# A convolution, Fourier and feed-forward block: the first normalisation's factors from transposes and statistics instructions, their placing by small DMAs, the gate products in five

## The chip, the cores and the metric

The kernel runs on one core of one Trainium2 chip. A core has five engines that run their own instruction queues in order and meet at semaphores: TensorE (PE, matrix products; weight loads are listed apart as PEld), VectorE (DVE), ScalarE (ACT), GpSimd (POOL) and SyncE (SP), which here only issues DMAs. SBUF is the working memory of 128 partitions, PSUM the memory that PE writes its results to. The metric is the device time of one execution in microseconds. The kernel before takes 7428.37 us, the median of 3 runs (7425.02 to 7429.1).

## The reference, cut to what matters

The input is 64 images of 96 channels and 56 x 56 pixels. Per image:

```
# layer 0: convolution
out = silu(bn(expand_w @ x))                  # 96 -> 192 channels
out = channel_shuffle(shift_groups(out), 4)
dw  = bn(depthwise3x3(out)) + bn(out * id_w)
out = silu(bn(dw))
se  = mean(out over pixels)                   # squeeze and excite, 12 groups
se  = sigmoid(exp_w . relu(red_w . se + red_b) + exp_b)
x   = silu(bn(proj_w @ (out * se)) + x)       # 192 -> 96 channels
# layer 1: tokens t = x as [3136 pixels, 96]
n   = (t - mean(t)) / sqrt(var(t) + 1e-5)     # first normalisation, over the channels
h   = relu(bn(n @ w1.T))                      # 192 channels
X   = fft(h over the pixels); complex relu with diagonal r, i; y = real(ifft)
t   = t + bn(y @ w2.T)
n   = (t - mean(t)) / sqrt(var(t) + 1e-5)     # second normalisation
t   = t + qlinear(relu(qlinear(n)))           # 96 -> 384 -> 96, rounded to 8 and 16 bits
```

The change concerns the first normalisation, the squeeze-and-excite gate and the order of all the work.

## The kernel before, in words

One image is one batch `b`. Its work is cut into small functions ("steps", listed in `STEPS`), each for one engine: `ea_mm` to `eb_ev` expand the channels from the padded image `x`, `dw_mm`/`dw_ev` and `lt`/`ls` do the depthwise convolution (on PE for 128 channels, on DVE for the other 64), `se1_mm` to `se2_pw` the gate, `pj_mm` to `pj_ev` the projection with the residual, which writes the tokens to one of three buffers `t`, channels on the partitions. `c_mm` to `sp_ev` are the first normalisation, `w1_mm`/`w1_ev` the first linear layer, `f1`, `f2`, `w2`, `i1`, `i2` the Fourier stage and its way back into `t`, `n_mm` to `x_ev` the second normalisation, `h_*` and `o_*` the feed-forward layer and the output.

The order is written out by hand in a table: `PLAN` gives every step and part of it a time within a batch, from about -152 to 302, and the program records all steps of all 64 batches sorted by `b * PERIOD + time`:

```
for _, b, k, i in sorted((b * PERIOD + when, b, k, i) for b in range(NB) ...):
    STEPS[k](b, i)
```

The times only sort. Each engine executes its own steps in that order, as early as their operands and buffers allow; a PERIOD of 116.13 doesn't hold the kernel to 116.13 us a batch. About four batches are in work at once.

Buffers that make steps wait: PSUM has two large buffers `psa`, used in turn by `w1`, `f1`, `f2`, `w2`, `i1`, `i2`, and four banks `psb` for all others; a bank is free again when the reader of its last tile is done. The image `x` (in SBUF) is one buffer, so rows of the next image are loaded (`x_in`, seven parts of eight rows, each two DMAs) when the projection has read the old ones. `rs_full`, the table of the factors, is one buffer too.

The first normalisation in the kernel before. Mean and factor are not applied to the tokens. `w1c` holds the weights with the centring folded in, the bias is in its row 48 (GAP), and row 48 of `t` gets the deviation of each token, so that the product plus bias comes out multiplied by the deviation; `w1_ev` multiplies by the reciprocal deviation from `rs_full`. For that:

- `c_mm` (L594, through `centred`, L575 to 583): for each of 7 groups of 4 x 112 tokens, a product of the tokens with the 96-column centring table, in two column tiles of 64 and 48 tokens. 56 products a batch.
- `c_sq` (L597, `squared`, L587) squares on ACT, `c_v` (L600, `variance`, L591 and L592) sums on DVE and scales, `c_pow` (L609) takes the power -1/2 on POOL, all by group.
- `sp_v` (L616) makes the deviations, for 16 and for 12 columns of 112 tokens. `sp_mm` turns them into rows by a product with the unit matrix `eye` (L623), and spreads the reciprocals over 128 partitions by two products with the selecting table `sel` (L626). `sp_ev` copies both out of PSUM and stores the deviations to row 48 of `t` with a small DMA (L635).

The second normalisation (`n_mm` to `n_x`) uses the same helpers `centred`, `squared` and `variance` and isn't changed.

The gate: `sums_of(b)` has nine columns of channel sums: four for each half of the image, for 128 channels in four groupings, and one for the other 64. `se1_mm` (L501) accumulates nine products with `rd_w`. `se2_mm` makes the 192 gate values in the layout that the projection wants, for 4 groupings of 32 channels, each four times over the partitions: 16 products of 32 rows (L516) and two of 64 (L524).

Of the kernel before, what the change touches and what calls it, by code (L numbers as in the profile page):

```python
# [15 lines left out]
C = 96  # L16
HW = 56
# [24 lines left out]
PERIOD = 116.1319138  # L42
PLAN = {
    "x_in": (-152.0645309, -141.2993712, -141.6679729, -127.3567477, -140.4175705, -140.8791946, -144.4420607),
    "ea_mm": (-135.7474068, -125.9928362, -122.8659980, -92.0913164, -104.6229276, -112.7267047, -105.2043967),
    "ea_ev": (-126.2515393, -125.9319230, -118.0983755, -90.4041115, -101.0728895, -111.5980423, -102.3613406),
    "eb_mm": (-111.6980332, -109.8791967, -100.7140648, -97.1962889, -100.1521321),
    "eb_ev": (-110.3732416, -105.7335079, -96.1257152, -94.4046805, -98.4601370),
    "dw_mm": (-82.7821446, -82.7811446, -81.0068981, -63.1375564, -61.9034126, -61.9024126),
    "dw_ev": (-77.0167479, -77.0167407, -77.0167341, -77.0167381, -60.0783737, -60.0901315, -61.6632225, -61.9014126),  # L50
    "lt": (
        -94.1171461, -91.0376475, -90.8110105, -84.2097398, -83.7232133, -81.4803127, -80.9974894, -76.5785475,
        -74.8117188,
    ),
    "ls": (-64.8543731,),
    "se1_mm": (-59.5055097,),
    "se1_ev": (-59.5045097,),
    "se2_mm": (-50.8239976,),
    "se2_ev": (-50.8229976,),
    "se2_th": (-49.7520464,),  # L60
    "se2_pw": (-44.5741770,),
    "pj_mm": (-42.5731636, -41.7287092, -36.7747065, -35.6782576),
    "pj_add": (
        -40.2650446, -40.2796225, -38.9333258, -40.2483174, -35.5690602, -35.5880423, -35.6772576, -33.4761964,
    ),
    "pj_ev": (-40.2419829, -40.2697824, -38.5536557, -39.8652465, -34.0027180, -34.0500919, -35.3385576, -32.9440877),
    "c_mm": (-25.3931448, -24.9391274, -22.9549349, -19.1090370, -21.8289396, -16.1784897, -12.8300748),
    "c_sq": (-24.0734158, -22.3310211, -21.2158857, -15.9717527, -16.5706079, -9.4527160, -10.1829185),
    "c_v": (-23.2641412, -18.5309510, -18.4395411, -12.1303106, -14.6345003, -8.6082441, -9.9996125),
    "c_pow": (-20.9452270, -13.7085425, -15.6301869, -11.4052805, -5.5266851, -7.5286825, -8.6183219),  # L70
    "sp_v": (-10.4956685, -0.4576308),
    "sp_mm": (-8.7178013, 0.9602487),
    "sp_ev": (-8.0803778, 4.1899488),
    "w1_mm": (1.8276103, -4.3293031, 1.4017277, 17.3741797, 5.8433199, 12.9915551, 9.4140075, 15.5299552),
    "w1_ev": (3.6555094, 1.6165891, 1.9120628, 20.7312269, 9.6265414, 15.0156650, 13.8227102, 19.8352916),
    "f1_mm": (21.4014670, 24.1096820, 21.6576037, 26.6862219, 27.4741769, 27.9467307),
    "f1_ev": (
        22.2675762, 22.3170374, 26.0226358, 25.8913366, 23.5344234, 24.6372460, 27.5678865, 27.6926244, 28.0977988,
        28.0983444, 28.8837920, 29.1288017,
    ),  # L80
    "f2_mm": (32.9716451, 29.2956139, 40.4533546, 44.1808546, 54.3439615, 55.8928972),
    "f2_u": (
        34.7148069, 35.1913156, 34.1757328, 34.5592467, 43.6172965, 44.2134504, 47.8768609, 48.4841614, 54.8402044,
        56.0332668, 59.7855946, 59.8827469,
    ),
    "f2_s": (
        37.7742909, 38.9626044, 36.3314048, 38.2311950, 49.1716883, 51.9368525, 50.9287577, 52.8460367, 57.5441738,
        59.9906303, 63.3144177, 64.6228680,
    ),
    "f2_r": (39.1150665, 38.5882242, 53.2778442, 54.0205100, 60.9052003, 68.4340083),  # L90
    "f2_p": (42.7834619, 39.8243535, 54.3731261, 54.5511382, 74.7679031, 77.0928815),
    "w2_mm": (65.3220254, 72.7056746, 74.7689031, 77.5437437),
    "w2_ev": (74.4448721, 74.9963870, 78.9222540, 80.2832661),
    "i1_mm": (80.9444124, 84.7640673, 88.5170591),
    "i1_ev": (82.2893126, 88.4629084, 91.9656135),
    "i2_mm": (95.7640245, 96.2774235, 108.3942264, 108.5026333),
    "i2_ev": (97.9070222, 99.2818561, 103.4147153, 107.9237827, 111.1146537, 111.4580718, 116.1401610, 115.7667382),
    "n_mm": (108.3281033, 107.0253359, 111.0518458, 120.4450658, 127.6246107, 127.0848414, 135.0039327),
    "n_sq": (108.8298534, 107.7986165, 117.6335593, 121.4070884, 128.9291689, 129.7921415, 135.5665766),
    "n_v": (109.1993497, 108.7476571, 118.3787911, 123.1793589, 128.9779128, 132.9514515, 137.6454231),  # L100
    "n_pow": (109.3967291, 109.1646949, 118.7377401, 123.8157957, 129.4982271, 133.4035466, 138.6999285),
    "n_x": (109.5403406, 109.6506044, 121.7562605, 124.9580100, 130.6758534, 134.0609417, 138.7110927),
    "x_mm": (109.8231134, 116.4694255, 122.0874878, 125.5477824, 134.5799192, 137.9526790, 139.7016670),
    "x_ev": (114.5600886, 118.9508230, 124.0625718, 126.2314751, 135.6759825, 140.9016708, 141.4110371),
    "h_mm": (
        141.6399550, 141.5117830, 141.4989540, 144.1173694, 144.1040402, 144.1151174, 156.6711686, 171.5607898,
        157.1121049, 172.3447607, 173.0555422, 181.3723226, 173.4712447, 192.1075898, 192.1283063, 199.7145424,
        199.3278846, 211.5886849, 203.8560342, 211.0696281, 205.6897160,
    ),
    "h_ev": (  # L110
        142.0485799, 142.2676534, 143.4387889, 146.2975891, 147.7127555, 145.5174570, 158.9476510, 171.7019227,
        158.8458276, 172.3457607, 176.0278841, 187.9388941, 188.9966021, 192.5081473, 192.7468496, 202.5167201,
        200.1670595, 212.5061452, 204.0408493, 216.0634498, 206.0694539,
    ),
    "h_b": (
        142.5658053, 143.5170823, 144.2148804, 151.8276368, 159.2819338, 152.3035773, 164.4059572, 171.8564611,
        162.0938148, 176.2691390, 188.9411972, 189.4355647, 190.4045783, 195.7931191, 194.6851523, 203.1792685,
        203.2135413, 217.0811781, 208.3076195, 221.1156131, 207.9598011,
    ),
    "h_q": (  # L120
        144.2114025, 144.2316186, 144.2262793, 153.1260293, 169.1449372, 154.5856829, 166.9828224, 177.8896970,
        168.8971320, 181.6666748, 191.8993395, 189.6006470, 193.7311756, 198.3792102, 198.6436559, 204.2406313,
        210.5749039, 220.8523876, 214.6332939, 223.7216018, 221.4920500,
    ),
    "o_mm": (144.4008021, 172.4113645, 192.8051961, 197.2106880, 201.6982825, 222.7674293, 226.6091401),
    "o_ev": (147.4341331, 172.4123645, 193.7082695, 205.9070152, 203.8978491, 223.5334454, 233.1469561),
    "o_b": (158.1581711, 179.3239824, 199.8546829, 224.1660979, 207.2258491, 223.5938860, 233.2919580),
    "o_f": (175.5923909, 198.5107896, 204.2384519, 228.4025252, 213.3142673, 272.9648091, 252.0032083),
    "o_st": (198.5980260, 220.5540600, 208.7628327, 254.9026667, 232.5265752, 302.3816775, 266.3798233),
# [4 lines left out]
def conv_attn_ffn(  # L134
# [30 lines left out]
    tab_sel: bass.AP,  # L165
# [82 lines left out]
    ep_w = load(exp_t, [24, MID], "ep_w")  # L248
# [5 lines left out]
    sel = load(tab_sel, [CP, 2, 128], "sel")  # L254
# [241 lines left out]

    def se1_mm(b, i):
        sums = held.pop(("sums", b))
        ps = psb.tile([128, 8], F32, tag="psb", name="ps_se")
        for i in range(9):  # L500
            nc.tensor.matmul(  # L501
                ps[0:24, 0:1], lhsT=rd_w[:, 4 if i == 8 else i % 4, :], rhs=sums[:, i : i + 1], start=i == 0, stop=i == 8
            )
        held["se", b] = ps
# [6 lines left out]
    def se2_mm(b, i):  # L511
        red = held["se", b]
        ps = psb.tile([128, NG], F32, tag="psb", name="ps_se2")
        for g in range(4):
            for j in range(4):
                nc.tensor.matmul(  # L516
                    ps[j * 32 : j * 32 + 32, g : g + 1],
                    lhsT=ep_w[:, g * 32 : g * 32 + 32],
                    rhs=red,
                    start=True,  # L520
                    stop=True,
                )
        for j in range(2):
            nc.tensor.matmul(ps[j * 64 : j * 64 + 64, 4:5], lhsT=ep_w[:, 128:MID], rhs=red, start=True, stop=True)  # L524
        held["se", b] = ps
# [68 lines left out]
    def c_mm(b, g):  # L594
        held["c", b, g] = centred(b, g, "ps_c")

    def c_sq(b, g):  # L597
        held["c", b, g] = squared(held["c", b, g])
# [528 lines left out]
```

## Time and profile before

| | |
|---|---|
| median of 3 runs | 7428.37 us (7425.02 to 7429.1) |
| span of the profiled execution, first to last instruction | 7414.7 us |
| mean granted TensorE clock | 0.993 |
| PE busy | 7188.3 us (97%) |
| DVE busy | 4842.3 us (65%) |
| ACT busy | 4641.4 us (63%) |
| POOL busy | 1589.9 us (21%) |
| moved by DMA | 185.34 MB, 25 GB/s |

The profile is of one execution. The times of one group of instructions are busy time (the union of their spans) and the mean of one. A matmul's span runs from its start to a modelled end, and the next one starts long before that end; so the time that a row of matmuls costs is read from the starts. In a line of the timeline, the first number is the start in us from the beginning of the span, the second the time to the end of the last instruction merged into the line, then engine, source line, operation, what is written and read, sizes, and how many instructions; in brackets the idle time before it and what ended it. In a line of the costliest groups, the numbers behind the bar are busy time in us, mean duration in ns, and idle time of the engine before these instructions, with what ended it. In a line of waits: who waited for whom, us in total, how often, the longest.

### The profile page before, as it was taken

What the parts mean: (1) busy time and instruction counts of PE and PEld (TensorE: products, weight loads), DVE (VectorE), ACT (ScalarE), POOL (GpSimd) and SP (SyncE); (2) the same over time, 40 slices, a digit from 0 to 9 for tenths busy, and PEclk for the clock granted to TensorE, in tenths of its full rate; (3) what the DMA queues carried; (4) which work ended last, traced back from release to release, by engine and by line L of the source; (5) the groups of instructions that cost most, each with busy time, mean ns of one, the idle gap of its engine ahead of it and who ended that gap; (6) DMA issues with size and microseconds to landing.
All of it is one profiled execution on the core that took longest, in us unless ns stands there. A gap on an engine that the chain in (4) does not pass through costs nothing.

```text
span 7414.7 us, 383547 instructions
## 1 busy us (share of the span) xinstructions
PE 7188.3 (97%) x177666; PEld 5229.7 (71%) x177666; DVE 4842.3 (65%) x8790; ACT 4641.4 (63%) x9806; POOL 1589.9 (21%) x1366
## 2 busy tenths in 40 slices
PE   7999999999999999999999999999999999999997
PEld 5777777777777777777777777777777777777775
DVE  5666667666666666666666666666666666666674
ACT  3566666566665666666656666566666666666665
POOL 1221222212212122122121221221212212212222
PEclk9999999999999999999999999999999999999998
DMA  2010110110101101011011011110110111101100
GB/s 52 18 28 20 28 27 19 28 24 23 28 20 28 26 20 28 21 27 28 18 29 26 20 28 23 25 27 19 30 26 20 28 23 24 28 20 28 27 20 21
DMA packets 424334, 185.34 MB, mean 25 GB/s; under 512 B 378786, under 2 KB 422042, under 8 KB 422474
## 3 DMA queue, kind: packets, MB, share of 16 engines
q1 hardware_dynamic: 420794, 159.01, 9.3%
q8 instruction: 1392, 22.81, 1.3%
q0 software_dynamic: 528, 1.50, 0.1%
q14 instruction: 212, 1.73, 0.1%
q10 hardware_dynamic: 1408, 0.28, 0.0%
HBM read 82.80 MB, written 77.07 MB: 22 GB/s over the span
## 4 chain that ended last, share of the span: by engine, by line
PE 93%; ACT 3%; issue 3%; DVE 1%; POOL 0%; DMA 0%; POOLq 0%; ACTq 0%; SPq 0%
PE ps_d L469 14%; PE psa L676 9%; PE psa L649 9%; PE ps_ea L406 5%; PE ps_eb L423 5%; PE psa L831 5%; PE ps_n L580 5%; PE ps_pj L555 5%; PE psa L768 5%; PE psa L809 4%; PE ps_c L580 4%; PE psa L703 4%; PE ps_h L888 4%; PE ps_o L910 3%; PE psa L713 3%
## 5 line engine op out<-in xcount | busy, mean ns | idle before, releaser
L926 POOL TENSOR_TENSOR o<-t,o 112x448 f32<-112x448 f32 x448 | 659.1, 1471 | 3629.9 <-DVE o L920 2280.0
L469 PE MATMUL ps_d<-e_a,diag 32*32 32x392 f32 x36864 | 1029.5, 498 | 0.7 <-ACT d L479 0.7
L898 DVE TENSOR_SCALAR y<-y,qb 128x448 f16<-128x448 f16 x1344 | 483.1, 384 | 761.5 <-ACT y L893 748.4
L491 DVE SCALAR_TENSOR_TENSOR d_last<-e_b,taps,d_last 128x1568 f32<-128x1568 f32 x512 | 972.5, 1899 | 9.3
L469 PEld LDWEIGHTS ps_d<-e_a,diag 32*32 32x32 f32 x36864 | 659.8, 103 | 299.6 <-issue 37.5
L591 DVE TENSOR_REDUCE v<-sq 112x4 f32<-112x384 f32 x896 | 490.6, 548 | 480.7 <-ACT sq L587 479.7
L893 ACT CAST y<-ps_h 128x448 f16<-128x448 f32 x1344 | 682.6, 543 | 165.7 <-PE ps_h L888 157.8
L860 POOL TENSOR_TENSOR rs<-v,mhalf 112x4 f32<-112x4 f32 x448 | 489.5, 1097 | 1264.2 <-DVE v L592 1264.2
L649 PEld LDWEIGHTS psa<-w1c,t 112*64 112x64 f32 x14336 | 609.0, 137 | 178.0 <-issue 86.4
L904 ACT CAST h<-y 128x448 fp8e5<-128x448 f16 x1344 | 733.0, 570 | 2.2 <-DVE y L898 2.0
L676 PEld LDWEIGHTS psa<-f_tab,buf_h 128*56 128x56 f32 x24576 | 650.4, 131 | 111.0 <-ACT buf_g L688 45.4
L649 PE MATMUL psa<-w1c,t 112*64 112x96 f32 x14336 | 688.4, 249 | 3.4 <-DVE buf_h L661 1.8
L676 PE MATMUL psa<-f_tab,buf_h 128*56 128x58 f32 x24576 | 675.6, 216 | 1.1 <-DVE buf_h L661 1.1
L609 POOL TENSOR_TENSOR rs<-v,mhalf 112x4 f32<-112x4 f32 x448 | 461.1, 1034 | 917.2 <-DVE v L592 763.3
L566 DVE TENSOR_TENSOR ps_pj<-ps_pj,x 112x392 f32<-112x392 f32 x512 | 260.6, 566 | 546.0 <-issue 326.1
L572 ACT ACTIVATE t<-ps_pj,pjbn_b 112x392 f32<-112x392 f32 x512 | 289.6, 621 | 413.5 <-DVE ps_pj L566 413.5
L661 DVE SCALAR_TENSOR_TENSOR buf_h<-psa,rs_full 128x768 f32<-128x768 f32 (+1 forms) x512 | 430.8, 852 | 148.7 <-PE psa L649 148.7
L688 ACT COPY buf_g<-psa 128x464 f32<-128x464 f32 x768 | 388.8, 551 | 186.4 <-PE psa L676 184.7
L411 ACT ACTIVATE e_a<-ps_ea 128x448 f32<-128x448 f32 x448 | 237.6, 551 | 427.3 <-PE ps_ea L406 427.2
L809 PE MATMUL psa<-inv_tab,buf_g 112*32 112x56 f32 x24576 | 373.3, 214 | 99.3 <-issue 97.5
L809 PEld LDWEIGHTS psa<-inv_tab,buf_g 112*32 112x32 f32 x24576 | 327.5, 110 | 197.5 <-issue 196.3
L866 DVE TENSOR_TENSOR xt<-ps_n,rs 112x384 fp8e5<-112x384 f32 x448 | 243.7, 556 | 315.8 <-POOL rs L860 311.4
(176 smaller groups left out, 12984.4 us busy)
## 6 DMA issues: line engine op xcount, KB each, us to landing
x<-in_x SPq DMA_DIRECT2D x896, 84.0 KB, 2.7
out_dram<-o SPq DMA_DIRECT2D x896, 84.0 KB, 2.1
l_tab<-in_tab_l SPq DMA_DIRECT2D x1, 1624.0 KB, 6.9
r_tab<-in_tab_r SPq DMA_DIRECT2D x1, 1568.0 KB
t<-dev_t SPq DMA_DIRECT2D x64, 7.0 KB, 1.8
t<-dev_t SPq DMA_DIRECT2D x64, 5.2 KB
ex_row_p<-in_expand_row POOLq DMA_DIRECT2D x1, 336.0 KB, 4.3
s_p<-in_bn POOLq DMA_DIRECT2D x1, 288.0 KB, 4.6
```

Source lines behind the costliest of these rows:

```text
L469: nc.tensor.matmul(pss[r][j * 32 : j * 32 + 32], lhsT=diag[pr, tap, :], rhs=e_a[pr, r0 : r0 + PJ, dx : dx + HW], start=tap == 0, stop=tap ...
L491: nc.vector.scalar_tensor_tensor(d_last, win, w, d_last, ALU.mult, ALU.add)
L580: nc.tensor.matmul(cen[c0:c1, k, 0:C], lhsT=t_of(b)[:, n0 + c0 : n0 + c1], rhs=center, start=True, stop=True)
L591: nc.vector.tensor_reduce(v, sq, AX.X, ALU.add)
L649: nc.tensor.matmul(ps[hc * 64 : hc * 64 + 64, k, 0:C], lhsT=t[:, n0 : n0 + 64], rhs=w1c[:, hc * C : hc * C + C], start=True, stop=True,)
L676: nc.tensor.matmul(ps[r * 64 : r * 64 + HW, k, 0 : 2 * NK], lhsT=buf_h[:, n0 : n0 + HW], rhs=f_tab[:, r, :], start=True, stop=True,)
L809: nc.tensor.matmul(ps[p0 : p0 + 32, k, 0:HW], lhsT=u_v[:, oh * 48 + o, :], rhs=inv_tab[:, r, :], start=True, stop=True,)
L860: nc.gpsimd.tensor_tensor(rs, held.pop(("nv", b, g)), mhalf[0:CP, 0:4], ALU.pow)
L893: nc.scalar.copy(y16, held.pop(("h", b, i)))
L898: nc.vector.tensor_scalar(y16, y16, qb1[:, i % 3 : i % 3 + 1], 0.0, ALU.add, ALU.max)
L904: nc.scalar.copy(held["h8", b, j][:, m, :], held.pop(("y", b, i)), saturate=False)
L926: nc.gpsimd.tensor_tensor(o32, rows, o16, ALU.add)
```

## The change

The work of the first normalisation up to the deviations is done by other instructions.

- `c_mm` transposes each block of 112 tokens with `eye` (PE's transpose), full width: 28 transposes a batch in place of 56 products.
- `c_st` (DVE) takes a `bn_stats` of each transposed block from PSUM: mean and summed squared deviation of two interleaved halves of the 96 channels. `c_sq` is gone.
- `c_v` and `c_pow` work on 16 and on 12 columns at once instead of 4 at a time. `c_v` combines the two halves in five DVE instructions.
- `sp_mm` only transposes the deviations. The reciprocals go to `rs_full` by four small DMAs of SP (`sp_ld`: 56 partitions by 16 or 12 columns), instead of two products with `sel` and a copy. `sp_ev` copies the deviations, and `sp_st` is their DMA to row 48 of `t`, now a step with a time of its own.
- The gate: `se0` (DVE) adds the four sums of the second half of the image to those of the first, so that `se1_mm` has five products. `ep_w` is laid out at the start as five sets of 128 columns, by six DMAs, so that `se2_mm` has five products.
- The table of times is new throughout; PERIOD is 116.13.

```
-PERIOD = 116.1319138
+PERIOD = 116.1300000
 PLAN = {
...
+    "se0": (-54.0101394,),
...
-    "c_mm": (-25.3931448, -24.9391274, -22.9549349, -19.1090370, -21.8289396, -16.1784897, -12.8300748),
-    "c_sq": (-24.0734158, -22.3310211, -21.2158857, -15.9717527, -16.5706079, -9.4527160, -10.1829185),
-    "c_v": (-23.2641412, -18.5309510, -18.4395411, -12.1303106, -14.6345003, -8.6082441, -9.9996125),
-    "c_pow": (-20.9452270, -13.7085425, -15.6301869, -11.4052805, -5.5266851, -7.5286825, -8.6183219),
-    "sp_v": (-10.4956685, -0.4576308),
-    "sp_mm": (-8.7178013, 0.9602487),
-    "sp_ev": (-8.0803778, 4.1899488),
+    "c_mm": (-35.6119810, -29.0676983, -29.6345782, -26.8057281, -22.1487238, -26.1960567, -30.3974314),
+    "c_st": (-31.4765613, -26.6880634, -29.1041470, -23.7402262, -18.3762517, -23.2171455, -29.2357042),
+    "c_v": (-22.8210727, -14.5557171),
+    "c_pow": (-22.5031762, -11.1238391),
+    "sp_v": (-11.6238887, -10.9528306),
+    "sp_ld": (-17.3508842, -2.9448996),
+    "sp_mm": (-8.1759444, -5.7622082),
+    "sp_ev": (-3.0651662, -2.7399409),
+    "sp_st": (-1.7476823, 0.8442928),
...
-    ep_w = load(exp_t, [24, MID], "ep_w")
+    ep_w = const.tile([24, NG, 128], F32, name="ep_w")
+    for j in range(4):
+        nc.sync.dma_start(
+            out=ep_w[:, 0:4, j * 32 : j * 32 + 32], in_=exp_t[:, 0:128].rearrange("r (g i) -> r g i", i=32)
+        )
+    for j in range(2):
+        nc.sync.dma_start(out=ep_w[:, 4, j * 64 : j * 64 + 64], in_=exp_t[:, 128:MID])
...
-    sel = load(tab_sel, [CP, 2, 128], "sel")
...
+    def se0(b, i):
+        sums = held["sums", b]
+        nc.vector.tensor_tensor(sums[:, 4:8], sums[:, 4:8], sums[:, 0:4], ALU.add)
+
     def se1_mm(b, i):
         sums = held.pop(("sums", b))
         ps = psb.tile([128, 8], F32, tag="psb", name="ps_se")
-        for i in range(9):
+        for i in range(NG):
             nc.tensor.matmul(
-                ps[0:24, 0:1], lhsT=rd_w[:, 4 if i == 8 else i % 4, :], rhs=sums[:, i : i + 1], start=i == 0, stop=i == 8
+                ps[0:24, 0:1], lhsT=rd_w[:, i, :], rhs=sums[:, 4 + i : 5 + i], start=i == 0, stop=i == 4
             )
...
     def se2_mm(b, i):
...
+        for g in range(NG):
+            nc.tensor.matmul(ps[:, g : g + 1], lhsT=ep_w[:, g, :], rhs=red, start=True, stop=True)
...
     def c_mm(b, g):
-        held["c", b, g] = centred(b, g, "ps_c")
-
-    def c_sq(b, g):
-        held["c", b, g] = squared(held["c", b, g])
-
-    def c_v(b, g):
+        ps = psb.tile([CP, 4, 128], F32, tag="psb", name="ps_c")
+        for k in range(4):
+            n0 = (g * 4 + k) * CP
+            nc.tensor.transpose(ps[:, k, 0:CP], t_of(b)[:, n0 : n0 + CP], eye)
+        held["c", b, g] = ps
+
+    def c_st(b, g):
+        if ("st", b) not in held:
+            held["st", b] = small.tile([CP, NJ, 6], F32, tag="st", name="st")
+        ps = held.pop(("c", b, g))
+        for k in range(4):
+            nc.vector.bn_stats(held["st", b][:, g * 4 + k, :], ps[:, k, :].rearrange("p (e o) -> p e o", e=2)[:, :, 0:48])
+
+    SP = ((0, 16), (16, 12))
+
+    def c_v(b, k):
...
+        v, _, d = held["v", b]
+        js = slice(SP[k][0], sum(SP[k]))
+        st = held["st", b][:, js, :]
+        nc.vector.tensor_tensor(d[:, js], st[:, :, 1], st[:, :, 4], ALU.subtract)
+        nc.vector.tensor_tensor(v[:, js], st[:, :, 2], st[:, :, 5], ALU.add)
+        nc.vector.scalar_tensor_tensor(d[:, js], d[:, js], C / 4.0, d[:, js], ALU.mult, ALU.mult)
+        nc.vector.tensor_tensor(v[:, js], v[:, js], d[:, js], ALU.add)
+        nc.vector.tensor_scalar(v[:, js], v[:, js], 1.0 / C, 1e-5, ALU.mult, ALU.add)
+
+    def c_pow(b, k):
         v, rs, _ = held["v", b]
-        js = slice(g * 4, g * 4 + 4)
-        nc.gpsimd.tensor_tensor(rs[:, js], v[:, js], mhalf[0:CP, 0:4], ALU.pow)
+        js = slice(SP[k][0], sum(SP[k]))
+        nc.gpsimd.tensor_tensor(rs[:, js], v[:, js], mhalf[0:CP, js], ALU.pow)
...
+    def sp_ld(b, k):
+        js = slice(SP[k][0], sum(SP[k]))
+        for h in range(2):
+            for d in range(2):
+                nc.sync.dma_start(
+                    out=rs_full[h * 64 : h * 64 + HW, d, js], in_=held["v", b][1][d * HW : d * HW + HW, js]
+                )
+
     def sp_mm(b, k):
...
-        nc.tensor.matmul(ps, lhsT=dev[:, js], rhs=eye, start=True, stop=True)
-        ps2 = psb.tile([128, 2, n], F32, tag="psb", name="ps_rs")
-        for d in range(2):
-            nc.tensor.matmul(ps2[:, d, :], lhsT=sel[:, d, :], rhs=rs[:, js], start=True, stop=True)
-        held["sp", b, k] = ps, ps2
+        nc.tensor.transpose(ps, held["v", b][2][:, j0 : j0 + n], eye)
+        held["sp", b, k] = ps
 
     def sp_ev(b, k):
...
-        nc.scalar.copy(dev_t, ps)
-        row = t_of(b)[GAP : GAP + 1, j0 * CP : (j0 + n) * CP].rearrange("p (j f) -> p j f", f=CP)
-        nc.sync.dma_start(out=row, in_=dev_t)
-        nc.scalar.copy(rs_full[:, :, j0 : j0 + n], ps2)
+        nc.scalar.copy(dev_t, held.pop(("sp", b, k)))
+        held["dev", b, k] = dev_t
+
+    def sp_st(b, k):
+        j0, n = SP[k]
+        row = t_of(b)[GAP : GAP + 1, j0 * CP : (j0 + n) * CP].rearrange("p (j f) -> p j f", f=CP)
+        nc.sync.dma_start(out=row, in_=held.pop(("dev", b, k)))
```

Where the steps around the change now stand, in the order of each queue (batches: b of this normalisation, b-1 and b-2 ahead, b+1 behind):

- PE: ... `w2_mm[0]`(b-1), `se1_mm`, `o_mm`, `h_mm`, `se2_mm`, `w2_mm[1]`, `pj_mm[0,1]`, `w2_mm[2,3]`, `pj_mm[2,3]`, `i1_mm[0]`, `h_mm`, `o_mm`, `h_mm`, `c_mm[0]`, `h_mm`, `i1_mm[1]`, `h_mm`, `c_mm[6,2]`, `h_mm`, `c_mm[1]`, `i1_mm[2]`, `o_mm`, `h_mm`, `c_mm[3,5]`, `i2_mm[0,1]`, `c_mm[4]`, two `h_mm`, `n_mm[0,1]`(b-1), `i2_mm[2]`, `ea_mm[1,0]`(b+1), `eb_mm[1,0]`, `ea_mm[2]`, `i2_mm[3]`, `sp_mm[0]`, `x_mm`, `x_mm`, `sp_mm[1]`, two `o_mm`, two `n_mm`, `w1_mm[0]`, ...
- POOL: `c_pow[0]`, `n_pow[0]`, `n_pow[1]`, `c_pow[1]`, two `o_f`, ...
- SP: `o_st[2]`, `sp_ld[0]`, `o_st[0]`, `x_in[3]`, `x_in[6]`, `sp_ld[1]`, `sp_st[0]`, `sp_st[1]`, `o_st[4]`, ...

## The prediction

> **What bounds the kernel now.** I read the page's first part (busy times) first, to see which engine could set the end:
>
> ```profile
> span 7414.7 us, 383547 instructions
> PE 7188.3 (97%) x177666; PEld 5229.7 (71%) x177666; DVE 4842.3 (65%) x8790; ACT 4641.4 (63%) x9806; POOL 1589.9 (21%) x1366
> ```
>
> TensorE is busy 97% of the span and nothing else is over 71%. A busy share alone would not prove it, since matmul ends are modelled, so next the busy times of one stretch in the middle of the run, about one batch long:
>
> ```profile
> 3000.00:3114.00 114.00, 112.12 (x2813) 81.54 (x2804) 76.01 (x139) 73.04 (x155) 24.58 (x22) 1.00 0.11 25
> ```
>
> Columns: length, then busy time of PE, weight loads, DVE, ACT and POOL, granted clock, DMA share, GB/s. PE idles 1.9 us in 114, at full clock; DVE and ACT have 38 and 41 us to spare. Then the costliest groups and the waits, for what ends the PE's idle time:
>
> ```profile
> L809 PE MATMUL psa<-inv_tab,buf_g 112*32 112x56 f32 x24576 | 373.3, 214 | 99.3 <-issue 97.5
> PEld ps_se L501 <- ACT d L479: 52.8, 127, 1.5
> ```
>
> The largest PE idle is 97.5 us of "issue" at L809 (1.5 us a batch), which no engine causes. So almost nothing that PE executes waits for another engine, and a batch costs what PE's instructions cost. Durations of overlapping matmuls (252 ns for one L580) can't be added up; a step's price on PE is the difference of starts in the timeline of PE:
>
> ```profile
> 3010.74 0.36 PE L501 MATMUL ps_se<-sums,rd_w 128*24 128x1 f32 x8
> 3011.30 0.41 PE L501 MATMUL ps_se<-sums,rd_w 128*24 128x1 f32 x10 [0.21 <-ACT d L479]
> 3011.64 0.86 PE L888 MATMUL ps_h<-xq,q 96*128 96x448 fp8e5 x3
> 3012.44 0.43 PE L516 MATMUL ps_se<-red,ep_w 24*32 24x1 f32 x32
> 3012.79 0.28 PE L524 MATMUL ps_se<-red,ep_w 24*64 24x1 f32 x4
> ...
> 3040.70 2.85 PE L580 MATMUL ps_c<-center,t 112*64 112x96 f32 x64
> 3043.48 0.55 PE L888 MATMUL ps_h<-xq,q 96*128 96x448 fp8e5 x2
> ...
> 3052.26 0.36 PE L623 MATMUL ps_dev<-eye,dev 112*16 112x112 f32 x2
> 3052.56 0.62 PE L626 MATMUL ps_rs<-rs,sel 112*128 112x16 f32 x4
> 3053.11 0.87 PE L580 MATMUL ps_n<-center,t 112*64 112x96 f32 x16
> ...
> 3087.03 0.59 PE L875 MATMUL ps_x<-eye,xt 112*96 112x112 fp8e5 x8
> 3087.55 0.96 PE L406 MATMUL ps_ea<-x,ex_w 112*32 112x448 f32 x8
> ```
>
> Each float32 product of the source is two instructions here. The same timeline 37 batches later has the first L501 at 7225.03: (7225.03 - 3010.74) / 37 = 113.9 us a batch. 64 of these are 7290; the other 125 us of the span are filling and draining. The span is 13.7 us short of the median of the runs, 7428.37; I carry that over unchanged.
>
> **What the skill says.** The Trainium skill, "TensorE: Matmul & The Clock Gate", Terms, gives loads and matmuls a transpose mode that is four times faster for float32. No run here shows a float32 transpose. Its section LDWEIGHTS (loading the stationary operand) prices a load by its columns, columns / 1.2 ns, whatever the rows: 107 ns for 128. The trace roughly agrees for float32: four L626, loads of 128 columns with 16 moving, take 3053.11 - 3052.56 = 0.55 us, 138 ns each. Its Part 4: PE-mode transpose has 275 ns for one in a kernel's context; I read that as a duration like L580's 252 ns, not a spacing.
>
> **The change part by part, per batch, on PE.**
>
> Centring (c_mm). Removed: 56 products, 112 instructions: 3043.48 - 3040.70 = 2.78 us for 64, and 2.13 for the other 48 (3047.74 to 3049.87), together 4.91. Added: 28 transposes, weights 112 columns of t, moving 112 columns of eye, full width, and in the compiled program one load and one matmul each instead of two. Low end: the nearest row in shape, L875, 8 in 0.52 us, 65 ns. High end: bound by a float32 load like L626, 138 x 112/128 = 120 ns. I take 80 ns, nearer the low end since the skill's factor four removes just what makes float32 dearer: 2.24 us. Saved 2.67 (1.55 to 3.09).
>
> Placing the factors (sp_mm). Removed: two L623 products and four L626: 0.30 + 0.55 us in the first half, and 0.29 + 0.55 in the second: 1.69. Added: two narrow transposes, at most one L623 instruction (0.15) each: 0.30. Saved 1.39.
>
> Gate. se1_mm's 9 products become 5: L501 took 0.69 us without its wait, so 0.38: saved 0.31. se2_mm's 18 small ones (0.35 + 0.21 us) become 5 with 128 weight columns in one row group, 10 instructions at L626's 138 ns: 1.38, a loss of 0.82. Net loss 0.51; se0 may remove L501's 0.21 us wait, as a w2_mm (2.3 us) now stands between the depthwise stage and se1_mm. I count a loss of 0.30 (0.1 to 0.5).
>
> Sum on PE: -2.67 - 1.39 + 0.30 = -3.76 us.
>
> The other engines, hidden as long as PE is the bound. ACT loses 7 squares (495 ns) and 2 copies: -3.8 us. DVE loses 7 reduces and 7 small operations (548 + 230 ns): -5.4; it gains 28 bn_stats, 10 operations of c_v and se0. For a bn_stats of 96 columns from PSUM I extrapolate L661 (953 ns at 768, 549 at 384): 247 ns alone, about 0.2 in a row; 28 are 5.6 to 6.9 us. With 11 small ones at about 0.2 DVE ends 2.4 to 3.7 us busier, 80 of some 110. POOL: seven powers of 1.03 us become two, of 16 and 12 columns: 1.03 us each if all is fixed cost, 4.1 and 3.1 if all is by column.
>
> The new order and its waits. I summed PE step times along the new order and looked at each wait. Gates: se2_mm to pj_mm has one w2_mm (2.3 us) in between instead of two; the chain gate, tanh, pw is 0.15 + 0.21 + 0.74 us and three handovers, below 2. pj_mm[3] to c_mm[0]: i1_mm, two h_mm and an o_mm, 2.9 us, against four additions and four activations in a pipeline, some 2.9: nothing to 0.3. sp_st lands (1.8 us) before w1_mm[0] behind 3.8 us of PE work; the small DMAs' rs_full is wanted later still.
>
> The tight one is SP's queue. sp_ld[0], four DMAs, waits for the power and stands ahead of o_st[0] and x_in[3]; eb_mm[0] of the next batch reads rows of x_in[3]. From the last transpose that c_v[0] needs to eb_mm[0], PE has 10.0 us: two i2_mm 2.9, c_mm 0.45, two h_mm 0.45, two n_mm 1.6, one i2_mm 1.45, two ea_mm 1.8, one eb_mm 1.45. The chain: two groups of bn_stats in DVE's queue 1.6, c_v 0.8, handovers 0.3, the power p, four issues at 0.45, o_st's two 0.9 (their rows in SP's timeline), x_in 0.45 and its landing 2.7: 8.55 + p. So p beyond 1.5 us makes PE wait by the excess, 2.6 us at the worst. I take p near 1.9, a wait of 0.4; behind it stand eb_mm[0], ea_mm[2] and all later PE work.
>
> The five extra loads of ep_w at the start (0.45 us each) lie under the 26 us that PE waits for w1s anyway.
>
> Total: -3.76 + 0.4 = -3.36 us a batch, times 64: -215. 7428 - 215 = 7213.
>
> **The rivals.** (1) A wait takes back most of it: p is by column, 4.1 us, and SP holds x_in[3] back by 2.6 instead of 0.4 us: +141, 7354. For it: POOL's 1.03 us for four columns of powers is 0.7 of what its plain addition of 448 columns takes (1.47), so the power may be dear per column; against it: a fixed part is likely.
>
> (2) Slower: DVE becomes the bound of the centring stage. Between c_mm[0] and n_mm[0] PE has 11.3 us; DVE must do 7 groups of four bn_stats plus 3.7 us of h_b, c_v and i2_ev, and PSUM buffers come free only after each group. At 0.2 us a bn_stats that is 9.3 us; each 0.1 more adds 2.8. It eats the gain when 28t + 3.7 exceeds 11.3 + 3.4, t = 0.39 us. At twice 0.25, 0.5 us: 17.7 - 11.3 = 6.4 us of wait against 3.4 saved, +3.0 a batch, 7620. Nothing in the profile speaks for a statistic that slow except that the trace has none.
>
> (3) The change doesn't do what it says: a transpose costs as much as the two column-tiled products that it replaces, 0.175 us. Then only sp_mm's gain remains, less the gate and the wait: -1.39 + 0.30 + 0.4 = -0.7, 7384. Above 0.20 us it would be slower.
>
> **How the numbers follow.** Forecast 0.66: with transposes at 65 to 120 ns and waits of 0 to 0.8 us, -4.2 to -1.8 a batch, 7160 to 7313. Rival 1 0.13; rival 3 0.07, a quarter of it past its break-even; rival 2, with any order in which new waits exceed the gain, 0.14. About 0.2% (15 us) is what a measurement of this kernel can tell from no change. Faster: 0.66 + 0.13 + 0.04 = 0.83; same 0.03; slower 0.14. The range goes from 7145 to 7390: forecast, rival 1 and most of rival 3.
>
> **What would show it.** Right: starts of 28 transposes 65 to 120 ns apart; two starts of L501's product a batch apart by about 110.5 us; PE idle still near 2 us a batch, DVE near 79, ACT near 69. ps_rs gone; se2_mm at about 1.4 us. Wrong: PE idle before ps_eb put down to the DMA of x, with powers of 2 us and more (rival 1); PE idle before ps_c, ps_n or ps_h put down to the statistics on DVE (rival 2); transposes spaced 175 ns or more (rival 3). If PE's idle time a batch grows by more than 3.4 us in any place, the sign is wrong.

## The result and the profile after

The changed kernel takes 7291.01 us, the median of four runs (7283.19 to 7303.33), against 7426.69 us before (7422.97 to 7429.1): a ratio of 0.9819, 95% interval 0.9805 to 0.9833, so 136 us faster. The forecast was 7213 us with a range of 7145 to 7390. The sign and the range hold; the likeliest time is 78 us short. The experiments show that this small distance hides two larger errors of opposite sign.

The page of the changed kernel, first the busy time of each engine:

```profile
span 7281.1 us, 367395 instructions
PE 6939.0 (95%) x169474; PEld 5096.4 (70%) x169474; DVE 4785.5 (66%) x10390; ACT 4485.2 (62%) x9232; POOL 1402.0 (19%) x1046
```

The same view by windows, for one batch in the middle of the run (length, then busy time of PE, weight loads, DVE, ACT and POOL, granted clock, DMA share, GB/s):

```profile
3000.00:3112.00 112.00, 106.79 (x2620) 78.29 (x2615) 73.16 (x156) 68.02 (x142) 21.47 (x16) 0.98 0.11 25
```

TensorE's busy share fell from 97% to 95%: it has less to do, and it waits more, 5.2 us in this batch against 1.9. DVE and ACT are no nearer to being the bound than before (73 and 68 us of 112). The granted clock (the share of TensorE's full clock that the profile shows as granted) of this window is 0.98; before it was 1.00. What the waits are is in the view of waits and, for the third line, in that of the groups:

```profile
PE ps_eb L430 <- DMA x<-in_x: 144.0, 63, 7.0
PE psa L789 <- DVE ue L768: 49.2, 63, 3.0
```

```profile
L830 PE MATMUL psa<-inv_tab,buf_g 112*32 112x56 f32 x24576 | 359.8, 214 | 29.5 <-issue 27.7 <-ACT buf_g L819 0.9
```

A wait for rows of x, 2.25 us a batch, which the kernel before did not have; a wait of w2_mm[0], 0.77 us a batch, also new; and the issue idle of i1_mm (idle time that nothing in the profile ends), L809 before, fell from 97.5 to 27.7 us. PE's timeline shows the changed instructions:

```profile
3002.23 0.60 PE L600 MATMUL ps_c<-eye,t 112*112 112x112 f32 x4
3002.66 0.54 PE L909 MATMUL ps_h<-xq,q 96*128 96x448 fp8e5 x2
...
3017.65 0.26 PE L645 MATMUL ps_dev<-eye,dev 112*16 112x112 f32 x1
3017.75 0.56 PE L896 MATMUL ps_x<-eye,xt 112*96 112x112 fp8e5 x8
...
3083.35 0.41 PE L512 MATMUL ps_se<-sums,rd_w 128*24 128x1 f32 x10
3083.68 0.78 PE L931 MATMUL ps_o<-h,q 128*112 128x448 fp8e5 x3
...
3084.58 1.27 PE L526 MATMUL ps_se<-red,ep_w 24*128 24x1 f32 x10
3085.78 1.53 PE L789 MATMUL psa<-w2a,buf_h 128*64 128x96 f32 x32
```

By starts: four transposes in 0.43 us, 108 ns each with the step to the next row; the deviations' transpose 0.10; five sums 0.33; the five wide gate products 3085.78 - 3084.58 = 1.20.

From here on a batch is the mean distance of the starts of pw's instruction (L540 before, L542 after) over all 63 pairs: 113.73 us before, 111.63 after. Costs of rows of products are sums over the whole trace, from start to start, divided by 64.

### Where the new wait comes from

The queues of POOL and SP in the same batch (a line of SP has the start of the issue, and the time to the end of the last issue merged into it):

```profile
3001.27 2.93 POOL L627 TENSOR_TENSOR rs<-v,mhalf 112x16 f32<-112x16 f32 x1 [5.54 <-DVE v L622]
```

```profile
3004.23 3.67 SPq L638 DMA_DIRECT2D rs_full<-rs  x4
3007.94 1.00 SPq L953 DMA_DIRECT2D out_dram<-o  x2
3008.99 2.02 SPq L194 DMA_DIRECT2D x<-in_x  x4
```

And PE, of the changed kernel, at the end of that chain:

```profile
3007.71 2.17 PE L430 MATMUL ps_eb<-x,ex_b 112*32 112x392 f32 x20
3012.33 1.18 PE L430 MATMUL ps_eb<-x,ex_b 112*32 112x392 f32 x10 [2.46 <-DMA x<-in_x]
```

The power ends at 3004.20, SP issues sp_ld[0] at once, then o_st[0], then x_in[3], whose two DMAs (the first two of the four in that line) are out at about 3010.0; eb_mm[0], four of whose instructions had run, goes on 2.35 us later. The power took 2.93 us for 16 columns (the old one 1.03 for four) and the four small DMAs 3.67 us to issue, 3.2 in most batches. From the start of the power to the end of the wait it is 11.06 us here and 10.96 on average over the 63 batches.

The wait costs more than its idle time. The windows around it, in the same columns as above:

```profile
3010.00:3012.30 2.30, 0.00 (x0) 0.00 (x0) 0.63 (x2) 0.00 (x0) 0.00 (x0) 1.00 0.78 150
3012.30:3014.00 1.70, 1.67 (x18) 0.81 (x20) 0.00 (x0) 0.00 (x0) 0.00 (x0) 0.84 0.06 5
3014.00:3016.00 2.00, 2.00 (x18) 0.55 (x14) 0.00 (x0) 0.37 (x1) 0.00 (x0) 0.50 0.04 3
3016.00:3018.00 2.00, 2.00 (x59) 1.94 (x56) 0.22 (x1) 1.07 (x4) 0.00 (x0) 0.78 0.00 0
```

When TensorE starts again its granted clock goes to 0.50 and comes back at about 3017. PE counts as busy in these windows, at half speed. In slices of 2 us from 200 to 7000 us, (1 - clock) times the length adds up to 59.6 us for the changed kernel, in 33 places that lose 1.7 or 3.4 us each, against 11.9 us in 7 places before.

### The profile page after: what moved, and what is told of

It is laid out like the page before. It is cut to its first block, busy times and chain, and to the rows that moved or that the text cites. A ratio compares the mean times of both kernels' runs of the same rounds, so it can differ in the third digit from the quotient of the medians.

```text
span 7281.1 us, 367395 instructions
## 1 busy us (share of the span) xinstructions
PE 6939.0 (95%) x169474; PEld 5096.4 (70%) x169474; DVE 4785.5 (66%) x10390; ACT 4485.2 (62%) x9232; POOL 1402.0 (19%) x1046
## 5 line engine op out<-in xcount | busy, mean ns | idle before, releaser
L947 POOL TENSOR_TENSOR o<-t,o 112x448 f32<-112x448 f32 x448 | 594.0, 1338 | 4801.1 <-ACT h L925 1846.0
L919 DVE TENSOR_SCALAR y<-y,qb 128x448 f16<-128x448 f16 x1344 | 446.7, 337 | 392.6 <-ACT y L914 390.9
L670 PE MATMUL psa<-w1c,t 112*64 112x96 f32 x14336 | 650.6, 247 | 4.6 <-DMA t<-dev_t 3.6
L430 PE MATMUL ps_eb<-x,ex_b 112*32 112x392 f32 x5120 | 455.8, 454 | 144.0 <-DMA x<-in_x 144.0
L865 DVE SCALAR_TENSOR_TENSOR t<-psa,bn2c_b,t 112x392 f32<-112x392 f32 x512 | 304.5, 620 | 400.2 <-PE psa L852 397.7
L881 POOL TENSOR_TENSOR rs<-v,mhalf 112x4 f32<-112x4 f32 x448 | 451.4, 1012 | 550.8 <-DVE v L594 489.1
L413 PE MATMUL ps_ea<-x,ex_w 112*32 112x448 f32 x3584 | 470.5, 574 | 5.3 <-ACT e_b L443 5.3
L749 ACT ACTIVATE ue<-psa,fa 128x448 f32<-128x448 f32 (+1 forms) x512 | 341.4, 692 | 198.1 <-DVE ue L768 123.2
L778 DVE SCALAR_TENSOR_TENSOR buf_h<-ue,s 128x448 f32<-128x448 f32 (+2 forms) x768 | 408.6, 581 | 80.4 <-ACT s L772 80.4
L430 PEld LDWEIGHTS ps_eb<-x,ex_b 112*32 112x32 f32 x5120 | 181.4, 110 | 397.7 <-issue 172.1
```

The source lines that it names most:

```text
L413: nc.tensor.matmul(ps[qs], lhsT=ex_w[:, qs], rhs=window(q, j * RPC, RPC), start=True, stop=True)
L430: nc.tensor.matmul(ps[p0 : p0 + 32], lhsT=ex_b[:, e, u].rearrange("p e i -> p (e i)"), rhs=window(2 * u + e, rows[h], n), start=e == 0, st ...
L670: nc.tensor.matmul(ps[hc * 64 : hc * 64 + 64, k, 0:C], lhsT=t[:, n0 : n0 + 64], rhs=w1c[:, hc * C : hc * C + C], start=True, stop=True,)
L778: nc.vector.scalar_tensor_tensor(pq[:, k0 : k0 + n, q * HW : q * HW + HW], ue[:, q, 0:n, :], 0.0, s[:, q, 0:n, :], ALU.max, op)
L881: nc.gpsimd.tensor_tensor(rs, held.pop(("nv", b, g)), mhalf[0:CP, 0:4], ALU.pow)
L919: nc.vector.tensor_scalar(y16, y16, qb1[:, i % 3 : i % 3 + 1], 0.0, ALU.add, ALU.max)
```

## The experiments

The theory after the result: the lost gain is the wait for x, and it comes from the order in SP's queue. The first four runs test this, the price of the transposes, and what the table of times alone does.

### x_first: x_in ahead of the small DMAs

```
-    "x_in": (..., -149.6507998, -126.6910437, -158.8298287, -141.2012121, -121.2167497),
+    "x_in": (..., -149.6507998, -133.6000000, -158.8298287, -141.2012121, -133.5000000),
```

> The changed kernel with two times of the table altered: x_in[3] and x_in[6] of the next image stand on SP's queue ahead of sp_ld[0] instead of behind it. Theory (the lost gain is a wait in SP's queue): TensorE's wait before eb_mm[0] for the DMA of x, 144 us in all, goes to almost nothing, and nothing else is late: 7291 - 144 = 7147 us, 7140 to 7200 if a part of it turns up elsewhere. Rival (the wait only moves: some other buffer or engine is late at the same place): the DMA wait goes, another of 1.5 us a batch and more comes in the next 20 us of TensorE's queue, 7240 to 7291.

Measured: 7045.77 us (7043.1 to 7050.38), ratio to before 0.9496 (0.9482 to 0.951). The waits of TensorE:

```profile
PE psa L789 <- DVE ue L768: 49.9, 64, 3.0
...
PE psa L830 <- issue: 24.5, 44, 1.6
```

The wait for x is gone and nothing took its place; the other two waits stand as they were. So the order in SP's queue is its cause. The gain is 245 us where the theory said 144: a batch is 107.87 us, 3.76 less than in the changed kernel. Of that, 2.25 is the idle time; about 1.0 is the clock (from 200 to 6800 us the changed kernel loses the whole 59.6 us, x_first 1.7 in one place; both lose more in their last 150 us, where the work runs out); and some 0.5 is the tail of the last product before the wait (it starts at 3009.38 and ends at 3009.87), which counts as busy while nothing starts behind it.

### spread_back: the reciprocals spread by products again

```
-                nc.sync.dma_start(out=rs_full[...], in_=held["v", b][1][...])     # sp_ld, four of them
+            nc.tensor.matmul(ps2[:, d, :], lhsT=sel[:, d, :], rhs=held["v", b][1][:, j0 : j0 + n], ...)  # sp_mm
+        nc.scalar.copy(rs_full[:, :, j0 : j0 + n], ps2)     # sp_ev
```

> The changed kernel, but the reciprocals go to rs_full as before: two products with sel and a copy on ACT in place of the four small DMAs; the transposed deviations stay. Theory (SP's queue): the products cost TensorE 1.4 us a batch (92 us), but with sp_ld the wait of 2.25 us a batch (144 us) is gone: 7291 + 92 - 144 = 7239, faster than with the small DMAs. Rival (the wait for x has another cause, as a slow landing): it stays and the products come on top, 7383.

Measured: 7098.39 us (7095.6 to 7107.2), ratio 0.957 (0.9554 to 0.9586). The direction is the theory's; the size again misses what the wait costs beyond its idle time. Without the small DMAs there is no wait for x, and a batch is 108.59 us, 0.72 more than in x_first. The rows of the four products cost 0.90 us a batch. In the order that the change chose, its small DMAs cost 193 us more than they save; in x_first's order they save 53.

### centre_back: products and squares again

```
-            nc.tensor.transpose(ps[:, k, 0:CP], t_of(b)[:, n0 : n0 + CP], eye)
+        held["c", b, g] = centred(b, g, "ps_c")
...
+        held["c", b, g] = squared(held["c", b, g])                                       # c_sq, new step on ACT
...
-            nc.vector.bn_stats(held["st", b][:, g * 4 + k, :], ps[:, k, :]...)
+        nc.vector.tensor_reduce(held["v", b][0][:, g * 4 : g * 4 + 4], held.pop(("c", b, g)), AX.X, ALU.add)
```

> The changed kernel, but the variance comes from centring products, squares on ACT and one reduce for each group on DVE, as before; powers, placing, gate and table stay as changed. Theory (TensorE is the bound, and 28 transposes at 107 ns stand against 5.2 us of products): 2.0 to 2.3 us more a batch on TensorE, 130 to 150 us: 7421 to 7441. Rival (VectorE's statistics hold the kernel back, so that the transposes brought little): not over 7330, since a reduce and no statistics leave VectorE 2 us less a batch.

Measured: 7357.13 us (7347.06 to 7365.71), ratio 0.9915 (0.9899 to 0.993): slower than the changed kernel, but by 66 us and not by 130 to 150. Neither expectation holds as a sum. The rows do what the theory says: c_mm costs 5.74 us a batch against 3.24, 2.50 more. But the wait for x shrinks with it:

```profile
PE ps_eb L431 <- DMA x<-in_x: 101.7, 63, 6.6
```

1.59 us of idle time a batch in place of 2.25, and with that the clock stays up (13.7 us lost instead of 59.6, 0.75 a batch): 0.66 + 0.75 come back, and 2.50 - 1.4 = 1.1 is near the 0.98 us by which the batch grew.

### table_alone: the old instructions in the new order

The kernel before with the new table; c_sq, c_v and c_pow stand at the statistics' times or shortly around them.

```
-    "c_mm": (-25.3931448, -24.9391274, ...),
+    "c_mm": (-35.6119810, -29.0676983, ...),
+    "c_v": (-31.4765613, -26.6880634, ...),      # c_st's times; all shared steps as in the changed kernel
```

> The kernel before with the changed kernel's table of times: all shared steps have their new times, c_sq, c_v and c_pow of each group stand where its statistics and shortly after are. No small DMAs, no transposes, nine and eighteen gate products. Theory (the instructions make the gain, the table moves waits): before's 7427, less about 1.1 us a batch that TensorE idled before i1_mm, plus about 0.75 for the new wait before w2_mm[0]: 7427 - 70 + 48 = 7405. Rival (the table makes most of the gain): 7330 or less. Second rival (the table alone loses, the instructions make up for it): 7460 or more.

Measured: 7272.39 us (7267.16 to 7280.29), ratio 0.9802 (0.9787 to 0.9816). The theory falls, the first rival holds: the new order alone makes a gain of 149 us with the old instructions (against 7421.41 us for the kernel before, measured beside it), 111.47 us a batch, 2.26 less. That is no less than the whole change gained: in its own order, the new instructions and the wait that they brought cancel. The rows against those of the kernel before, us a batch by starts (the whole trace divided by 64, so with filling and draining):

```
                  before  table_alone
i1_mm              7.18      5.67
w1_mm             10.32      9.66
eb_mm              6.14      5.53
n_mm               5.52      4.92
o_mm               4.87      4.46
se1_mm             0.96      0.57
h_mm               5.11      6.64   (1.1 of it before w2_mm[0]'s new wait)
all others        75.22     75.54
```

Rows of the same instructions became cheaper. se1_mm's part is mostly a wait that went (TensorE idled 16.4 us for d before it, now 1.8), and o_mm's was not traced. For the others, two things can be read in the traces. i1_mm's issue idle fell:

```profile
L809 PE MATMUL psa<-inv_tab,buf_g 112*32 112x56 f32 x24576 | 349.7, 214 | 25.2 <-issue 23.1 <-ACT sq L587 1.1 <-ACT buf_g L798 0.9
```

And rows with the same column tiles stand together. In the kernel before, eb_mm stands alone among w1_mm parts, 3067.81 - 3066.36 = 1.45 us for 16:

```profile
3065.56 0.87 PE L580 MATMUL ps_n<-center,t 112*64 112x96 f32 x16
3066.36 1.52 PE L423 MATMUL ps_eb<-x,ex_b 112*32 112x392 f32 x16
3067.81 1.54 PE L649 MATMUL psa<-w1c,t 112*64 112x96 f32 x32
```

In table_alone the last three eb_mm are one row, 2.86 us for 48, of which 16 are of the short form (0.34 us in the kernel before):

```profile
3007.51 3.04 PE L423 MATMUL ps_eb<-x,ex_b 112*32 112x392 f32 x48
3010.36 2.43 PE L406 MATMUL ps_ea<-x,ex_w 112*32 112x448 f32 x24
```

n_mm shows the same: its 16 products take 0.80 us ahead of an eb_mm (3065.56 to 3066.36), and in table_alone 0.66 on average between two w1_mm, which have the same column tiles, with no wait in either place. The next two runs undo each of the two, the distance of i1_mm's parts and the company of eb_mm, in x_first.

### i1_close and eb_apart: the order of rows

```
-    "i1_mm": (77.0638854, 81.5405180, 88.4270933),
+    "i1_mm": (77.0638854, 80.4000000, 83.0000000),                    # i1_close
-    "eb_mm": (..., -105.1668674, -103.9800216, -103.7810025),
+    "eb_mm": (..., -109.1300000, -105.8300000, -103.7810025),         # eb_apart, eb_ev moved with it
```

> x_first (7046 us) with the three parts of i1_mm closer together, as in the kernel before: the transposes no longer stand between them, and only about 1 us of other TensorE work does. Theory (rows of 128 products at 13 ns each run ahead of their instructions' supply, and slower work in between lets it catch up): TensorE's issue idle in i1_mm goes from 0.4 to about 1.5 us a batch, and its row time from 5.9 to about 7.1: +70 us, 7090 to 7125. Rival (the idle time of the kernel before had another cause than the distance): 7046 to 7060.

> x_first (7046 us) with eb_mm[2] and eb_mm[3] put among the w1_mm parts, as in the kernel before, instead of beside eb_mm[4] and three ea_mm. Theory (each change between rows of products with different column tiles costs 0.1 to 0.5 us, since the next row doesn't overlap with the last; the new table has fewer such changes): an eb_mm alone takes 1.45 us where two beside each other took 2.5, and each w1_mm cut off by it 0.15 more: +0.7 us a batch, 7075 to 7100. Rival (the order of rows doesn't matter, the gain of the table was waits alone): 7040 to 7055.

Measured: i1_close 7252.48 us (7249.52 to 7263.37), ratio 0.9765 (0.9751 to 0.978); eb_apart 7213.99 us (7211.48 to 7217.6), ratio 0.9711 (0.9697 to 0.9726). Both are slower than x_first by far more than expected, 207 and 168 us. First i1_close, then eb_apart:

```profile
PE psa L830 <- issue: 102.8, 111, 1.7
PE ps_o L931 <- ACT h L925: 59.5, 69, 1.8
PE psa L852 <- ACT buf_h L841: 53.1, 62, 1.6
```

```profile
PE psa L697 <- DVE buf_h L682: 83.0, 63, 1.6
...
PE ps_eb L430 <- DVE xt L887: 32.3, 62, 0.8
```

The part in question came as expected: with the i1_mm close together the issue idle is back, 102.8 us, and the row takes 7.27 us a batch (5.87 in x_first, 7.18 in the kernel before); with eb_mm apart the rows of eb_mm cost 0.35 more and those of w1_mm 0.19. The rest is mostly waits that the moves made, since nothing else was moved to fit: o_mm and i2_mm wait for ACT, f1_mm for w1_ev, an eb_mm for its buffer. In i1_close some 24 us more are half clock (25.6 us lost from 200 to 6800 us, against 1.7 in x_first).

Between two parts of i1_mm lie 0.9 to 1.1 us of other work before, 0.7 to 1.1 in i1_close, 1.6 to 1.9 in x_first and 2.3 to 2.9 in table_alone. i1_close changes with the distance also what lies between; but in table_alone centring products lie there in place of the transposes, and the issue idle is as low (0.36 us a batch, 0.38 in x_first). So the distance is what these runs point to, and neighbours of the same tiling are worth some 0.55 us a batch here; that a longer gap lets the supply of instructions catch up is an explanation and was not shown itself.

### power_twice: the power in the chain

```
+        for _ in range(2 - k):
             nc.gpsimd.tensor_tensor(rs[:, js], v[:, js], mhalf[0:CP, js], ALU.pow)
```

> The changed kernel, with the first power of a batch (112 x 16) computed twice in a row; the table is unaltered. Theory (bn_stats, power, small DMAs and x_in[3] are one chain that TensorE waits for): the chain grows by one power, 2.93 us a batch, so TensorE's idle time before eb_mm[0] grows from 2.25 to 5.2 us a batch and the clock drops to half after nearly every one of these waits instead of after half of them: 2.9 to 3.8 us a batch, 7475 to 7535. Rival (the power is hidden, SP or the DMA engines alone are late): 7291 to 7310.

Measured: 7549.8 us (7539.37 to 7553.73), ratio 1.0161 (1.0146 to 1.0176), a little over the range. The power is in the chain, as the theory has it, and not hidden:

```profile
PE ps_eb L430 <- DMA x<-in_x: 252.2, 63, 10.1
...
PE ps_eb L430 <- DVE xt L888: 49.4, 58, 1.2
```

Idle time before eb_mm is 3.94 + 0.77 us a batch, 4.7 where 5.2 was expected; the second term is DVE's work for the second normalisation, whose own powers (n_pow) queue behind the doubled one on POOL. The clock loses 168.8 us in the run where the changed kernel loses 59.6. A batch is 4.0 us longer, against 2.5 more idle and 1.8 more at a low clock, which together are a little too much. One power of 2.95 us costs 259 us here, and would cost 189 by its length alone.

### small_gate, ue_split and both

On x_first: the second gate product in its old form with the five sums kept (small_gate); the tile ue in two halves (ue_split); and both.

```
-            nc.tensor.matmul(ps[:, g : g + 1], lhsT=ep_w[:, g, :], rhs=red, ...)      # five
+                nc.tensor.matmul(ps[j * 32 : j * 32 + 32, g : g + 1], lhsT=ep_w[:, g * 32 : g * 32 + 32], rhs=red, ...)
...
-            held["ue", b, i] = work.tile([128, 2, 8, HW], F32, tag="ue", name="ue")
+            held["ue", b, i] = [work.tile([128, 8, HW], F32, tag=f"ue_{p}", name=f"ue_{p}") for p in range(2)]
```

> x_first (7046 us) with the second gate product as before, 16 products of 32 columns and two of 64, and the first one with five sums as changed. Theory (the five wide products are the dearer form, 1.22 us against 0.58): -0.64 us a batch, 7005. Rival (the time is the gate's chain of handovers, not its products): 7040 to 7050.

> x_first (7046 us) with the tile ue of the Fourier stage cut into two tiles, one for each of its halves; in f2_s the half q then waits for the activation of its own half only. Theory (f2_s of part 4 starts 0.6 us late because it waits for both activations, and w2_mm[0] waits for its end, 0.75 us of idle time and about 1.1 by starts a batch): 0.6 us a batch comes back on TensorE, -40 us, 6985 to 7015. Rival (f2_s waits for its own half already, or something else in w2_mm[0]'s way ends as late): 7040 to 7050.

> x_first with the small gate products (7004 us) and with the halves of ue in tiles of their own. Theory (TensorE is the bound and the two gains are at different places in its queue): they add up, 7004 less what ue_split gains over x_first; with the 40 us expected there, 6965. Rival (one gain uncovers a wait that takes the other's place): 7000 or more.

Measured: small_gate 7004.29 us (6998.41 to 7010.56), ratio 0.9432 (0.9416 to 0.9447), as the theory says. Its timeline:

```profile
3061.35 0.43 PE L521 MATMUL ps_se<-red,ep_w 24*32 24x1 f32 x32
3061.70 0.28 PE L529 MATMUL ps_se<-red,ep_w 24*64 24x1 f32 x4
```

Eighteen small products take 0.59 us a batch, five wide ones 1.24: fewer instructions were the dearer form.

ue_split 7056.56 us (7053.99 to 7057.34), ratio 0.9506 (0.9493 to 0.9519), no gain, as the rival says. The batch is that of x_first, 107.88 us against 107.87; the 11 us on top come from the start, where TensorE waits 40.1 us for w1s instead of 25.6 (the edit also moves a buffer that is used there). f2_s still starts when both activations are done, and w2_mm[0] waits as before. DVE's and ACT's timelines:

```profile
3093.99 0.62 DVE L765 SCALAR_TENSOR_TENSOR s<-psa,fb,ue 128x392 f32<-128x392 f32 x1 [0.89 <-ACT ue L749]
```

```profile
3092.71 1.25 ACT L749 ACTIVATE ue<-psa,fb 128x392 f32<-128x392 f32 x2 [0.29 <-PE psa L734]
```

Two activations end at 3093.96, and 0.03 us later DVE starts. Since the tile was not the reason, why it waits for the second one stays open.

both 7001.91 us (6999.57 to 7002.83), ratio 0.9433 (0.942 to 0.9446): no different from small_gate; its batch is 107.14 us for 107.24, and it too starts later, by 6 us. small_gate and both, at 7002 to 7004, are faster than the changed kernel by 287 us and more.

## Why the prediction was right and wrong

The account of a batch, from the four runs that stand on each other: 113.73 before, -2.26 by the new order with the old instructions (table_alone), -3.60 by the new instructions without the wait (x_first), +3.76 by the wait (the changed kernel): 111.63. (Taken in this sequence of runs; another sequence would divide it a little differently.) The forecast was 0, -3.76, +0.4. The sum for the instructions was right within 0.2, and the two terms of order and waiting both missed, in opposite directions: -2.26 that was not foreseen, and +3.36 on top of the 0.4. That the likeliest time came within 78 us is therefore luck; with the wait alone mis-sized it would have missed by some 215 us, an estimate from 3.36 times 64.

- **Centring, -2.67.** Before to x_first the row goes from 5.54 to 3.26, -2.28; against the same order, 5.77 to 3.26, -2.51. The 4.91 us of the old row came from one batch; over the trace it is 5.54. A transpose starts 96 ns after the last, and with the steps to the next rows the 28 cost 116 each (3.26 us), in the bounds of 65 to 120, but above the 80 taken. One instruction pair in place of two is seen; beyond that the 96 ns stand against 120 scaled from L626's plain products. One lasts 259 ns, so the 275 ns were rightly read as a duration. The low end, L875, was the wrong neighbour: the Trainium skill, "TensorE: Matmul & The Clock Gate", section LDWEIGHTS (loading the stationary operand), has columns / 1.2 ns for a load, an estimated 93 ns for 112 columns, which agrees with 96. A load's price was used for the high end only, taken from L626, whose 138 ns lie above the page's 107 for 128 columns. Rival 3 (0.175 us) is out.
- **Placing the factors, -1.39.** 1.69 to 0.33 in x_first: -1.36, as forecast; at the same order, 1.55 to 0.33, -1.22.
- **Gate, +0.30.** 1.54 to 1.59 us from before to x_first, +0.05, since se1_mm's wait went too; at the same order, 1.16 to 1.59, +0.43. A size, in the right direction: five wide products 1.24, not 1.38.
- **The wait for x, +0.4.** This step failed, though its mechanism, its place and the sign of the risk were right: it is rival 1. The chain behind the start of the power was put at p + 5.85 with p = 1.9, and took 11.06 us (3001.27 to 3012.33). The power was 2.93, 1.03 over; the four issues 3.67, not four times 0.45, 1.87 over; x_in's two DMAs about 1.0 for 0.45; the landing 2.35 for 2.7. With 0.1 for o_st, and the gaps between issues, the chain behind the start of the power is 3.3 us longer. Ahead of it the chain was 0.8 shorter, 1.9 us from the last transposes (their row ends at 2999.34) where 2.7 was allowed, and TensorE had the 10.0 us of other work (2999.34 to 3009.38; the parts listed add up to 10.1). So the wait is 2.5 longer than 0.4, and by starts it is 2.95 (3009.38 to 3012.33). The issue price came from SP's row for DMAs of other shapes, and no bound was put around it; the bounds were on p alone. The trace before had a nearer price: the small store of deviations (L635), also from one SBUF tile to another, took 0.51 to 0.81 us to issue. And a wait was priced by its idle time, although half clock follows it. Rival 1's 2.6 us would have been near 4 us with that, by an estimate from the 1.0 of clock and 0.5 of tail in x_first.
- **The table, 0.** "I summed PE step times along the new order" took each row's time from its old neighbours. So it missed -2.26 us: i1_mm's issue idle, dismissed as a wait "which no engine causes" and carried over unchanged, and the changes between tilings. How the 2.26 divides is shown only in part: 1.51 is i1_mm's row, 0.55 came back in eb_apart's rows, and new waits run against it. The new wait of w2_mm[0] was not foreseen either.
- **DVE as the bound (rival 2)** is out: four bn_stats of 96 columns from PSUM take some 0.66 us (two groups of four merge to 1.42 us), 0.165 each, less than the 0.2 taken and far from 0.39. DVE went from 76.0 to 73.2 us in its window instead of to 79.
- **What would show it.** Period about 110.5: it is 111.63. PE idle near 2 us: 5.2. Wait before ps_eb with powers of 2 us and more: seen, as the sign of rival 1.

## What to carry to other kernels

When a step is moved to DMAs, list what stands behind them in the same issuing queue and bound the issue time as well as the compute time ahead of it; the fix may be two numbers in an order. A wait of TensorE of about 2 us cost its length here and, in about half of the cases, 1.7 us more of half clock, so removing one is worth more than the view of waits says. Before costing a new order as neutral, look at rows of small products, at what stands next to them and between them: a new order of the same instructions gained 2% here.

## What the runs showed that was not expected

- **The clock after short waits.** Of the 63 waits for x in the changed kernel, 34 were followed by a stretch at half clock, with idle times from 1.82 us up; the 12 waits under 1.82 us never were, and between 1.82 and 2.9 us it varies. The Trainium skill, "TensorE: Matmul & The Clock Gate", Part 1: The HAM clock gate, describes half rate after an idle window of about 3.4 us, free-running. The free-running window agrees: all changes of the clock in this trace stand on one grid of 3.413 us, and each place loses 1.7 us, half of one such window, or 3.4. That the whole window must be idle does not: with TensorE's idle time counted in each window (200 to 6900 us), the 33 that turned the clock from full to half had 1.82 us or more of it, and none with more than 1.83 kept full clock; in power_twice the border lies between 1.83 and 1.86. So a wait of some 2 us costs clock when most of it falls into one window, which accounts for the variation. The idle time of the profile is not the whole measure: in i1_close the border is at 1.63 us, and three of the seven places before follow windows with 0.3 us of idle time.
- **Power by column.** POOL's power on 112 partitions takes 1.01 us for 4 columns, 2.27 for 12 and 2.93 for 16: about 0.16 us a column on top of some 0.37. The two powers of a batch take less than the seven before (5.2 against 7.2 us), but the first result comes later.
- **Issues of small DMAs.** Four DMAs of 56 rows by 64 bytes took SP 3.67 us in the batch shown and 3.2 in most, about 0.8 each, while two DMAs of x or of the output take 0.8 to 1.0.
